# Layer 0's weight folds in fp32r halves with GpSimd butterflies, and down weights re-laid inside SBUF

## The chip, the cores and the metric

The kernel runs on one core of one Trainium2 chip. The metric is the device time of one execution in microseconds. The engines are TensorE (PE; PEld is its weight load), VectorE (DVE), ScalarE (ACT), GpSimd (POOL) and SyncE (SP), whose queue issues nearly all DMAs.

## The reference

Two layers over x of 4 x 512 tokens x 512 features. Each layer is x + s * silu(f), where s is an attention and f a feed-forward network, both of the normalised x.

- Layer 0, attention: 32 query heads of 16, 8 key heads, softmax over 512 keys.
- Layer 0, feed-forward (the part the change touches), with H a normalised Walsh-Hadamard transform:

```python
x = fwht(x * SU_ug) / SCALE                        # 512 features
x_up = x @ W_up.T * (Wscale_ug[:INTER] * SCALE)    # INTER = 2048
x_gate = x @ W_gate.T * (Wscale_ug[INTER:] * SCALE)
x = silu(x_gate) * x_up
x = fwht(x * SU_dp) / SCALE                        # 2048 features
x = x @ W_down.T * (Wscale_dp * SCALE)
```

- Layer 1: a gated delta-rule recurrence over 6 heads of 64, and a feed-forward network with the signs of its weights.

The kernel does not transform the activations of layer 0's feed-forward network. It folds the transforms into the weights once, at the start: H512 diag(SU_ug) into gate and up, H2048 diag(SU_dp) and the scales into down.

## The kernel before

**The stream.** Layer 0 is one stream of units `u` (line 532). Unit u holds maxima of scores (`maxima`, PE L418, DVE reduce L419), exponentials 11 units later (`exps`, PE L439, ACT L441), weight work from the table `early`, and from u = 16 on two halves of the feed-forward network (`half`, so `gate_up` at L326 or `down` at L344). Eight units are one set of four heads; before a set begins, `set_queries` brings its queries into `qT` by four DMAs (L405). `values` follows each set (L449 to L473). A batch has 64 units: 32 with `gate_up`, 32 with `down`. The tile framework's scheduler decides the final order of the instructions on each engine; each engine then runs its own queue in order and waits on semaphores. Layer 1 follows with its own stages.

**Gate and up weights.** There are 16 pieces n (eight groups of 256 columns, gate and up in turn). `load_raw(n)` loads 128 x 4 x 256 fp32 (three buffers `raw`). `mix(n, 0)` and `mix(n, 1)` are butterflies over the four 128-row blocks, each an add (L52) and a subtract (L53) of 128 x 512, on DVE. `fold(n, j)` multiplies two blocks each by the fp32 matrix `hs`, which is the 128-point transform times SU_ug (made by L516 to L519), and splits the result into two fp32r parts: the rounded one on ACT (L256), the rest on DVE (L257). The parts `fo` serve batch 0's `gate_up` directly and are stored to `wS` in DRAM (L262) for the other batches. `fold(n, 1)` also issues the load of raw n + 3. Chunk c of `gate_up` uses half of pieces 2(c // 2) and 2(c // 2) + 1. Its up half goes through ACT into `hT` (L336) and is multiplied there on POOL (L337).

**Down weights.** 16 tiles `stage[q]` of 128 x 512, in the buffers that `hT` uses later, hold rows 16p + q of W_down.T. `mix_down(q)` multiplies one by the 16-step part of the transform, `h16`, with a plain fp32 product (L270), copies it back (L271) and writes it to DRAM as rows of `wdt` (L272). After the last one, four DMAs read `wdt` into `wdn` with other rows on the partitions (L275). `fold_down(a)` is another fp32 product with `hmat` (L281) and a scaling on DVE (L282).

Of the kernel before, what the change touches and what calls it, by code (L numbers as in the profile page):

```python
# [10 lines left out]
F32 = mybir.dt.float32  # L11
F32R = mybir.dt.float32r
AF = mybir.ActivationFunctionType
ALU = mybir.AluOpType
# [4 lines left out]
P = 128  # L19
NB, SEQ, DM = 4, 512, 512  # L20
NT = NB * SEQ // P
TB = SEQ // P
KC = DM // P
FF = 2048
NI = FF // P
# [8 lines left out]
def kernel(ctx: ExitStack, tc: tile.TileContext, i: dict, out: bass.AP):  # L34
    nc = tc.nc

    def new(pool, shape, dtype, tag, **kw):
        return pool.tile(shape, dtype, tag=tag, name=tag, **kw)
# [9 lines left out]
    def butterfly(eng, dst, src, dim, h, pin=lambda ins: ins):  # L48

        s = src.rearrange("p (n two h) f -> p n two h f", two=2, h=h)  # L50
        d = dst.rearrange("p (n two h) f -> p n two h f", two=2, h=h)
        pin(eng.tensor_tensor(d[:, :, 0], s[:, :, 0], s[:, :, 1], ALU.add))  # L52
        pin(eng.tensor_tensor(d[:, :, 1], s[:, :, 0], s[:, :, 1], ALU.subtract))  # L53
# [24 lines left out]
    dram = ctx.enter_context(tc.tile_pool(name="dram", bufs=1, space=DRAM))  # L78
# [7 lines left out]
    sum_d = new(dram, [NB, HG, 4, SEQ], F32, "sum_d")  # L86
    rec_d = new(dram, [NB, HG, 4, SEQ], F32, "rec_d")

    wdt = new(dram, [FF, DM], F32, "wdt")

    identf = new(cst, [P, P], F32, "identf")
    make_identity(nc, identf)
# [8 lines left out]
    if True:  # L101
# [5 lines left out]
        bmm = l0.enter_context(tc.tile_pool(name="bmm", bufs=3, space=PSUM, side="right"))  # L107
        awp = l0.enter_context(tc.tile_pool(name="awp", bufs=1, side="right"))
        hp = l0.enter_context(tc.tile_pool(name="hp", bufs=2, side="right"))
        a0 = top.enter_context(tc.tile_pool(name="a0", bufs=1, side="right"))  # L110

        wdn = new(awp, [P, NI, DM], F32, "wdn")
        su_ug = new(awp, [P, KC], F32, "su_ug")
# [17 lines left out]
        inorder = tc.keep_in_program_order  # L131
# [31 lines left out]
        CQ = 2 * P  # L163
        raws, fos = {}, {}

        def load_raw(n):
            q, m = n // 2, n % 2
            raws[n] = new(a0, [P, KC, CQ], F32, "raw", bufs=3)
            nc.sync.dma_start(
                raws[n], i[("w_gateT", "w_upT")[m]][:, ts(q, CQ)].rearrange("(k p) n -> p k n", p=P)  # L170
            )
# [11 lines left out]

        stage = [new(hp, [P, DM], F32, "hT", bufs=16) for _ in range(NI)]
        for q in range(NI):
            if q in (0, 6, 12):
                load_raw(q // 6)
            nc.sync.dma_start(stage[q], i["w_downT"].rearrange("(p q) n -> q p n", q=NI)[q])


# [16 lines left out]

        hmat = identf
        for h in (8, 16, 32, 64, 1, 2, 4):
            nxt = new(a0 if h == 64 else awp, [P, P], F32, "h16" if h == 64 else "hmat", bufs=1 if h == 64 else 2)  # L210
            butterfly(nc.vector, nxt.unsqueeze(2), hmat.unsqueeze(2), P, h, inorder)
            hmat = nxt
            if h == 64:
                h16 = nxt
        inorder(nc.vector.tensor_reduce(
            mrow, identf.rearrange("p (j d) -> p j d", d=32)[:, :, 0:2], AX.XY, ALU.add
        ))
# [12 lines left out]
        def scales():  # L230
            inorder(nc.vector.tensor_scalar(hwg, wsc[:, 0, :], 0.5 / DM**0.5, None, ALU.mult))
            inorder(nc.vector.tensor_tensor(cdn, wsc[:, 0, :], wsc[:, 1, :], ALU.mult))
            nc.vector.tensor_tensor(cdn, cdn, su_dp, ALU.mult)
            nc.vector.tensor_scalar(cdn, cdn, 0.5 / DM / FF**0.5, None, ALU.mult)
# [3 lines left out]
        tmps = {}  # L238

        def mix(n, stage):  # L240
            if stage == 0:
                tmps[n] = new(a0, [P, KC, CQ], F32, "tmp")
                butterfly(nc.vector, tmps[n], raws[n], KC, 1)
            else:
                butterfly(nc.vector, raws[n], tmps[n], KC, 2)

        def fold(n, j):
            q, m = n // 2, n % 2
            if j == 0:
                fos[n] = new(a0, [P, 2, 2, KC, P], F32R, "fo", bufs=3)  # L250
            ph = new(bmm, [P, 2, CQ], F32, "mm")
            for k in range(2):
                nc.tensor.matmul(ph[:, k, :], hs[:, 2 * j + k, :], raws[n][:, 2 * j + k, :], start=True, stop=True)
            ph = ph.rearrange("p k (c n) -> p c k n", n=P)
            hi, lo = fos[n][:, :, 0, 2 * j : 2 * j + 2, :], fos[n][:, :, 1, 2 * j : 2 * j + 2, :]
            nc.scalar.copy(hi, ph)  # L256
            nc.vector.tensor_tensor(lo, ph, hi, ALU.subtract)  # L257
            if j == 0:
                return
            if n + 3 < FF // P:  # L260
                load_raw(n + 3)
            nc.sync.dma_start(  # L262
                wS[ts(q, 2), m].rearrange("c p h k n -> p c (h k n)"),
                fos[n].bitcast(F32).rearrange("p c h k n -> p c (h k n)"),
            )


        def mix_down(q):
            ph = new(bmm, [P, DM], F32, "mm")
            nc.tensor.matmul(ph, h16, stage[q], start=True, stop=True)  # L270
            nc.scalar.copy(stage[q], ph)  # L271
            nc.sync.dma_start(wdt.rearrange("(p q) n -> q p n", q=NI)[q], stage[q])  # L272
            if q == NI - 1:
                for o in range(4):
                    nc.sync.dma_start(  # L275
                        wdn[:, ts(o, 4), :], wdt[ts(o, DM), :].rearrange("(a p) n -> p a n", p=P)
                    )

        def fold_down(a):
            ph = misc()  # L280
            nc.tensor.matmul(ph, hmat, wdn[:, a, :], start=True, stop=True)  # L281
            nc.vector.scalar_tensor_tensor(wdn[:, a, :], ph, cdn[:, a : a + 1], drow, ALU.mult, ALU.mult)  # L282

        vps, kTs, oTs, hTs, g0s, wcs, ths = {}, {}, {}, {}, {}, {}, {}
# [72 lines left out]
        def misc(dtype=F32):  # L357

            return new(bpy, [P, SEQ], dtype, "y") if piece[0] % 64 < 32 else new(bmm, [P, SEQ], dtype, "mm")
# [10 lines left out]
        def halves(u):  # L370

            return 2 * (min(max(u, LATE), NU) - LATE) + max(u - NU, 0)
# [129 lines left out]
        def half(h):  # L502
            piece[0] = h // 2
            ffn(h // 2, h % 2)
# [5 lines left out]
        nc.sync.dma_start(drow, i["wsc_dp"].to_broadcast([P, DM]))  # L510
        nc.sync.dma_start(wo, i["wo0"].rearrange("(k p) n -> p k n", p=P))

        ph = new(bmm, [P, KC, P], F32, "mm")
        for k in range(KC):
            hk = new(a0, [P, P], F32, "hk", bufs=1)
            inorder(nc.vector.tensor_scalar(hk, hmat, su_ug[:, k : k + 1], None, ALU.mult))  # L516
            nc.tensor.transpose(ph[:, k, :], hk, identf)
        hs = new(a0, [P, KC, P], F32, "hs")
        nc.scalar.copy(hs, ph)  # L519

        scales()

        early = {}
        for n in range(FF // P):
            u = LATE + 2 * n - 4
            for d, f in ((-3, lambda n=n: mix(n, 0)), (-2, lambda n=n: mix(n, 1)),
                         (0, lambda n=n: fold(n, 0)), (1, lambda n=n: fold(n, 1))):
                early.setdefault(u + d, []).append(f)
        for q in range(NI):
# [2 lines left out]
        for u in range(NU + LAG + 1):  # L532
            b, r = u // 64, u % 64
            v = u - LATE
            piece[0] = halves(u) // 2
            if v == 32:
                top.close()
                zp.append(l0.enter_context(tc.tile_pool(name="zp", bufs=2, side="right")))
            if 0 < u - LAG <= NU and (u - LAG) % 8 == 0:
                values((u - LAG) // 8 - 1)  # L540
            if u < NU:
                maxima(u)
            if 0 <= u - LAG < NU:
                exps(u - LAG)
            for f in early.get(u, ()):
                f()
            for h in range(halves(u), halves(u + 1)):
                half(h)
            if u % 8 == 7 and u < NU:
                max_rows(u // 8)  # L550
            if u % 32 in (22, 23) and u + 10 < NU:
                queries((u + 10) // 64, (u + 10) % 64 // 32, u % 32 - 22)
            if u % 8 == 0 and u + 8 < NU:
                set_queries(u // 8 + 1)
            if 16 <= v < 16 + NI:
                fold_down(v - 16)
            if 0 < b < NB and r in (18, 19, 20, 21):
                layer_sum(b - 1, r - 18)
            if 0 < b < NB and r in (25, 26, 28, 29):
                norm1(b - 1, (25, 26, 28, 29).index(r))  # L560
            if b + 1 < NB:
                if r == 34:
                    load_x(b + 1)
                if r in (43, 44, 45, 46):
                    stats0(b + 1, r - 43)
                if r == 49:
                    norm0(b + 1)
                if r == 52:
                    keys_values(b + 1)
# [284 lines left out]
    total, done, n = sum(x[0] for x in steps), 0.0, 0  # L854
# [53 lines left out]
    raws = {}  # L908
# [492 lines left out]
    n = 0  # L1401
# [56 lines left out]
```

## Time and profile before

| | us |
|---|---|
| median of 3 runs | 1493.79 (1490.02 to 1494.76) |
| span of the profiled execution, first to last instruction | 1492.3 |
| median less that span | 1.5 |
| first maxima product (L418) | 18.4 |
| first product of gate_up (L326) | 43.1 |
| last product of a gate or up fold (L253) | 164.9 |
| first product of down (L344) | 183.7 |

No separate device time is listed for the profiled execution, so its span is set beside the median. An engine's busy time is a mean over stages with different limits; what an edit of the first 165 us is worth is read from that stage. Times in the lists below the page count from the span's start. A transfer's row on SPq is the time that its issue holds the queue, not the time until it lands. One fp32 product appears as two records.

### The profile page before, as it was taken

Reading aid. Unit: us, or ns where it says so; the run is one execution under the profiler, and the core shown is the slowest. Engines: PE = TensorE matmul, PEld = TensorE weight load, DVE = VectorE, ACT = ScalarE, POOL = GpSimd, SP = SyncE. Lnnn points to the kernel's source line nnn. Section 1 sums busy time; section 2 is a strip of 40 time slices with the busy share of each in tenths; the row PEclk is TensorE's granted clock in tenths of the full one; section 3 lists DMA queues with packets and bytes.
Section 4 is the critical chain, followed back from the end, with each engine's and each line's share of the span. In section 5 each row is a group of like instructions: output and inputs, shape, how many; then the busy total and the mean of one; then the engine's idle time right before and its main releaser. Section 6 shows DMA issues by size and latency. Waiting matters only on the chain. (4 is left out here: it accounts for less than half of the span.)

```text
span 1492.3 us, 22700 instructions
## 1 busy us (share of the span) xinstructions
PE 1429.4 (96%) x8144; PEld 855.6 (57%) x8144; DVE 1035.8 (69%) x1863; ACT 709.6 (48%) x1046; POOL 313.5 (21%) x304
## 2 busy tenths in 40 slices
PE   7999999999999999999999899999999999999998
PEld 3565533555335553356434576787568766776675
DVE  7999755765557655666525869768975799477746
ACT  4655554666446664466552434434353344323433
POOL 1112100322003220033100330045112531052001
PEclk9999999999999999999999999999999999999989
DMA  8865410475105741166103553434453354425532
GB/s 307 322 220 194 149 29 16 149 237 190 27 21 190 231 149 28 36 212 225 56 20 103 160 146 101 116 92 147 134 151 103 91 161 135 126 73 150 162 83 96
DMA packets 201793, 199.11 MB, mean 133 GB/s; under 512 B 65520, under 2 KB 153040, under 8 KB 200784
## 3 DMA queue, kind: packets, MB, share of 16 engines
q1 hardware_dynamic: 198624, 196.29, 41.9%
q10 hardware_dynamic: 3056, 1.37, 0.4%
q8 instruction: 64, 1.05, 0.3%
q14 instruction: 49, 0.40, 0.1%
HBM read 146.80 MB, written 46.19 MB: 129 GB/s over the span
## 5 line engine op out<-in xcount | busy, mean ns | idle before, releaser
L419 DVE TENSOR_REDUCE nmx<-sc 128x2 f32<-128x1024 f32 x256 | 312.3, 1220 | 159.1 <-PE st L439 147.3
L441 ACT ACTIVATE pe<-st 128x1024 f16<-128x1024 f32 x256 | 262.6, 1026 | 143.4 <-PE st L439 141.6
L344 PE MATMUL y<-wdn,hT 128*128 128x512 f32 x512 | 253.3, 617 | 3.0 <-DVE g L348 1.7
L326 PE MATMUL mm<-xr,wc 128*128 128x512 f32 x768 | 206.8, 410 | 0.0
L326 PEld LDWEIGHTS mm<-xr,wc 128*128 128x128 f32 x768 | 137.4, 189 | 48.4 <-issue 21.8
L337 POOL TENSOR_TENSOR hT<-hT,th 128x512 f32<-128x512 f32 x64 | 84.2, 1316 | 319.2 <-ACT hT L336 309.0
L344 PEld LDWEIGHTS y<-wdn,hT 128*128 128x128 f32 x512 | 87.0, 189 | 96.0 <-issue 88.5
L711 PE MATMUL pu<-xn1T,wp 128*128 128x512 f32 x288 | 129.9, 594 | 0.0
L941 PE MATMUL ph<-xsh,sg 128*128 128x512 f32 x256 | 113.0, 441 | 5.6 <-ACT sg L926 5.3
L418 PE MATMUL sc<-kT,qT 32*128 32x512 f16 x512 | 102.5, 385 | 7.8 <-DVE nmx L419 7.4
L926 ACT ACTIVATE sg<-sw 128x512 fp32r<-128x512 f32 x128 | 79.5, 625 | 55.2 <-PE y L972 32.2
L941 PE MATMUL ph<-xsl,sg 128*128 128x512 f32 x256 | 104.1, 407 | 0.7 <-DVE xsl L901 0.7
L418 PEld LDWEIGHTS <-qT 32*128 32x128 f16 x512 | 26.2, 91 | 131.8 <-issue 127.9
L465 POOL TENSOR_TENSOR oT<-os,sm 128x512 f16<-128x512 f32 x32 | 41.5, 1298 | 285.9 <-DMA sm<-rec_d 248.8
L439 PE MATMUL st<-qm,kT 32*128 32x512 f16 x512 | 100.0, 384 | 0.3 <-ACT pe L441 0.3
L946 ACT ACTIVATE hT<-ph,upsc 128x512 f32<-128x512 f32 x64 | 43.8, 685 | 94.3 <-PE ph L941 94.1
L711 PEld LDWEIGHTS pu<-xn1T,wp 128*128 128x128 f32 x288 | 54.0, 191 | 56.6 <-issue 54.8
L972 PE MATMUL y<-sg,hsh 128*128 128x512 f32 x256 | 83.0, 432 | 0.7 <-ACT sg L926 0.7
L1019 POOL TENSOR_TENSOR gm<-g,le 128x384 fp32r<-128x384 f32 x64 | 57.8, 921 | 83.0 <-PE pu L1020 52.0
L326 PE MATMUL mm<-xr,fo 128*128 128x512 f32 x256 | 73.2, 420 | 0.9 <-DVE fo L257 0.9
L972 PE MATMUL y<-sg,hsl 128*128 128x512 f32 x256 | 73.5, 400 | 0.0
L332 ACT ACTIVATE th<-mm,hwg 128x512 f32<-128x512 f32 x64 | 44.0, 688 | 56.0 <-PE mm L326 56.0
(302 smaller groups left out, 2370.2 us busy)
## 6 DMA issues: line engine op xcount, KB each, us to landing
wc<-wS SPq DMA_DIRECT2D x96, 512.0 KB
wS<-fo SPq DMA_DIRECT2D x16, 1024.0 KB
sw<-in_upT SPq DMA_DIRECT2D x64, 256.0 KB
sw<-in_downT SPq DMA_DIRECT2D x64, 256.0 KB
sm<-rec_d SPq DMA_DIRECT2D x128, 64.0 KB
raw<-in_w_gateT SPq DMA_DIRECT2D x8, 512.0 KB
hT<-in_w_downT SPq DMA_DIRECT2D x16, 256.0 KB
raw<-in_w_upT SPq DMA_DIRECT2D x8, 512.0 KB
```

The costliest lines, as they stand in the source:

```text
L326: nc.tensor.matmul(pgs[m], wcs[b, c, m][:, h, k, :], xrs[b][:, k, :], start=(k + h == 0), stop=(k == KC - 1 and h == 1))
L337: nc.gpsimd.tensor_tensor(hT, hT, ths[b, c], ALU.mult)
L344: nc.tensor.matmul(ys[t], hTs[b, c][:, ts(t, P)], wdn[:, c, :], start=(c == 0), stop=(c == NI - 1))
L418: nc.tensor.matmul(sc[:, j, :], qTs[n][rows, ts(t, P)], kTs[b, g // 4][rows, :], start=True, stop=True)
L419: nc.vector.tensor_reduce(nmxs[n][:, t, 2 * pr : 2 * pr + 2], sc, AX.X, ALU.max, negate=True)
L439: nc.tensor.matmul(st[:, j, :], kTs[b, g // 4][rows, ts(k, P)], qms[n][rows, :], start=True, stop=True)
L441: nc.scalar.activation(pes[u], st, AF.Exp)
L711: nc.tensor.matmul(pp, wps[b, n][:, k, 0:P], xn1Ts[b][:, k, :], start=(k == 0), stop=(k == KC - 1))
L926: tc.keep_in_program_order(nc.scalar.activation(sgs[b, c, m], raws[b, c, m], AF.Sign))
L941: ins = nc.tensor.matmul(ph, sgs[b, c, 0][:, ts(k, P)], xss[b][n][:, k, :], start=(k + n == 0), stop=(k == KC - 1 and n == 1))
L972: ins = nc.tensor.matmul(yss[b][t], hss[b, c][n][:, ts(t, P)], sgs[b, c, 1], start=(c + n == 0), stop=(c == NI - 1 and n == 1))
L1019: nc.gpsimd.tensor_tensor(gm, bc_in(s["g2"][:, t, u, x], P), bc_mid(le, 3), ALU.mult)
```

## The change

Three things change in layer 0's weight preparation.

1. The folds of gate and up, `mix_down` and `fold_down` use two fp32r products each in place of one fp32 product: `halves_of` splits the data into a rounded part on ACT and the rest (on DVE for gate and up, on POOL for down), and both are multiplied by an fp32r matrix of plus and minus one. SU_ug is applied where the fold is split (ACT with a scale, DVE with scalar_tensor_tensor, one block at a time), so `hs` and its four transposes go.
2. The butterflies of gate and up run on POOL. `raw` has two buffers and not three; raw n + 2 is loaded by `part_raw(n, 1)`.
3. The down weights change their rows by 128 transfers from SBUF to SBUF, eight per `mix_down`, each from 16 partitions into one. `fold_down` is spread over units from u = 24.

```diff
-            raws[n] = new(a0, [P, KC, CQ], F32, "raw", bufs=3)
+            raws[n] = new(a0, [P, KC, CQ], F32, "raw", bufs=2)
...
-            if q in (0, 6, 12):
-                load_raw(q // 6)
+            if q in (0, 8):
+                load_raw(q // 8)
...
         def mix(n, stage):
             if stage == 0:
                 tmps[n] = new(a0, [P, KC, CQ], F32, "tmp")
-                butterfly(nc.vector, tmps[n], raws[n], KC, 1)
+                butterfly(nc.gpsimd, tmps[n], raws[n], KC, 1)
             else:
-                butterfly(nc.vector, raws[n], tmps[n], KC, 2)
+                butterfly(nc.gpsimd, raws[n], tmps[n], KC, 2)
+
+        def halves_of(src, eng):
+            rh = new(a0, [P, 2, DM], F32R, "rh", bufs=2)
+            hi = rh[:, 0]
+            nc.scalar.copy(hi, src)
+            eng.tensor_tensor(rh[:, 1], src, hi, ALU.subtract)
+            return rh
+
+        rhs = {}
+
+        def part_raw(n, j):
+            rhs[n, j] = halves_of(raws[n][:, 2 * j : 2 * j + 2, :].rearrange("p k n -> p (k n)"), nc.vector)
+            if j == 1 and n + 2 < FF // P:
+                load_raw(n + 2)
...
             for k in range(2):
-                nc.tensor.matmul(ph[:, k, :], hs[:, 2 * j + k, :], raws[n][:, 2 * j + k, :], start=True, stop=True)
-            ph = ph.rearrange("p k (c n) -> p c k n", n=P)
-            hi, lo = fos[n][:, :, 0, 2 * j : 2 * j + 2, :], fos[n][:, :, 1, 2 * j : 2 * j + 2, :]
-            nc.scalar.copy(hi, ph)
-            nc.vector.tensor_tensor(lo, ph, hi, ALU.subtract)
+                for h in range(2):
+                    nc.tensor.matmul(ph[:, k, :], hmr, rhs[n, j][:, h, ts(k, CQ)], start=(h == 0), stop=(h == 1))
+            for k in range(2):
+                kk = 2 * j + k
+                src = ph[:, k, :].rearrange("p (c n) -> p c n", n=P)
+                hi = fos[n][:, :, 0, kk, :]
+                nc.scalar.activation(hi, src, AF.Copy, scale=su_ug[:, kk : kk + 1])
+                nc.vector.scalar_tensor_tensor(
+                    fos[n][:, :, 1, kk, :], src, su_ug[:, kk : kk + 1], hi, ALU.mult, ALU.subtract
+                )
             if j == 0:
                 return
-            if n + 3 < FF // P:
-                load_raw(n + 3)
...
         def mix_down(q):
+            rh = halves_of(stage[q], nc.gpsimd)
             ph = new(bmm, [P, DM], F32, "mm")
-            nc.tensor.matmul(ph, h16, stage[q], start=True, stop=True)
+            for h in range(2):
+                nc.tensor.matmul(ph, h16r, rh[:, h], start=(h == 0), stop=(h == 1))
             nc.scalar.copy(stage[q], ph)
-            nc.sync.dma_start(wdt.rearrange("(p q) n -> q p n", q=NI)[q], stage[q])
-            if q == NI - 1:
-                for o in range(4):
-                    nc.sync.dma_start(
-                        wdn[:, ts(o, 4), :], wdt[ts(o, DM), :].rearrange("(a p) n -> p a n", p=P)
-                    )
+            for r in range(P // NI):
+                nc.sync.dma_start(wdn[r * NI + q : r * NI + q + 1, :, :], stage[q][r : P : P // NI, :])

         def fold_down(a):
+            rh = halves_of(wdn[:, a, :], nc.gpsimd)
             ph = misc()
-            nc.tensor.matmul(ph, hmat, wdn[:, a, :], start=True, stop=True)
+            for h in range(2):
+                nc.tensor.matmul(ph, hmr, rh[:, h], start=(h == 0), stop=(h == 1))
...
+                         (-1, lambda n=n: part_raw(n, 0)), (0, lambda n=n: part_raw(n, 1)),
...
-            if 16 <= v < 16 + NI:
-                fold_down(v - 16)
+            for a in range(NI):
+                if v == 8 + 3 * a // 2:
+                    fold_down(a)
```

More of the change, by code (lines that the diff above doesn't have):

```diff
@@ L87 @@
     rec_d = new(dram, [NB, HG, 4, SEQ], F32, "rec_d")
-    wdt = new(dram, [FF, DM], F32, "wdt")
     identf = new(cst, [P, P], F32, "identf")
@@ L209 @@
         for h in (8, 16, 32, 64, 1, 2, 4):
-            nxt = new(a0 if h == 64 else awp, [P, P], F32, "h16" if h == 64 else "hmat", bufs=1 if h == 64 else 2)
+            nxt = new(a0, [P, P], F32, "hmat", bufs=2)
             butterfly(nc.vector, nxt.unsqueeze(2), hmat.unsqueeze(2), P, h, inorder)
@@ L213 @@
             if h == 64:
-                h16 = nxt
+                h16r = new(a0, [P, P], F32R, "h16r")
+                inorder(nc.vector.tensor_copy(h16r, nxt))
+        hmr = new(a0, [P, P], F32R, "hmr")
+        inorder(nc.vector.tensor_copy(hmr, hmat))
         inorder(nc.vector.tensor_reduce(
@@ L511 @@
         nc.sync.dma_start(wo, i["wo0"].rearrange("(k p) n -> p k n", p=P))
[L513 to L519, printed above, removed]
         scales()
```

## The prediction

> **What bounds the kernel now.** I read the page's busy line and slices first, then the same engines by stage, since the edit touches only the first 165 us.
>
> ```profile
> PE 1429.4 (96%) x8144; PEld 855.6 (57%) x8144; DVE 1035.8 (69%) x1863; ACT 709.6 (48%) x1046; POOL 313.5 (21%) x304
> ```
> ```profile
> 20.00:43.00 23.00, 23.00 (x81) 10.34 (x80) 19.42 (x31) 13.06 (x23) 0.00 (x0) 1.00 0.89 321
> 43.00:165.00 122.00, 114.52 (x570) 69.56 (x568) 117.45 (x167) 69.88 (x97) 22.48 (x16) 1.00 0.62 226
> ```
> The columns of the second fence are stage, length, then busy time (and instructions) of PE, PEld, DVE, ACT and POOL, clock, DMA share, GB/s. From the first weight product (18.4 us) PE is hardly idle, DVE is 96% busy during the folds, and POOL does almost nothing. So a change that frees PE and DVE could pay, if what takes over can keep up. What takes over is POOL and the SP queue, and their prices stand in these rows (groups of the window 43 to 181, one row of POOL's and one of DVE's timeline, SP's timeline, one line's instructions, one stage):
>
> ```profile
> L326 PE MATMUL mm<-xr,fo 128*128 128x512 f32 x256 | 73.2, 420 | 0.9 <-DVE fo L257 0.9
> L253 PE MATMUL mm<-raw,hs 128*128 128x256 f32 x111 | 32.7, 408 | 1.5 <-DVE fo L257 1.5
> ```
> ```profile
> 53.60 1.27 POOL L337 TENSOR_TENSOR hT<-hT,th 128x512 f32<-128x512 f32 x1 [46.87 <-ACT hT L336]
> ```
> ```profile
> 53.70 1.72 DVE L53 TENSOR_TENSOR tmp<-raw 128x512 f32<-128x512 f32 x1
> 56.48 0.68 DVE L52 TENSOR_TENSOR raw<-tmp 128x512 f32<-128x512 f32 x1
> ```
> ```profile
> 23.27 0.34 SPq L272 DMA_DIRECT2D wdt<-hT  x1
> 23.89 2.42 SPq L405 DMA_DIRECT2D qT<-qd  x4
> 26.41 4.82 SPq L272 DMA_DIRECT2D wdt<-hT  x8
> 31.32 2.43 SPq L405 DMA_DIRECT2D qT<-qd  x4
> ...
> 36.49 0.38 SPq L169 DMA_DIRECT2D raw<-in_w_upT  x1
> ```
> ```profile
> L405 SPq DMA_DIRECT2D qT<-qd x124: 507/540/1587, 23.9 to 710.4; - x124
> ```
> ```profile
> 228.50:231.00 2.50, 2.50 (x10) 0.86 (x9) 1.21 (x2) 0.67 (x1) 0.00 (x0) 1.00 0.11 25
> ```
> To see: a POOL tensor_tensor of 128x512 takes 1.27 us, DVE's 0.68; a DVE one on two SBUF tiles that meets a POOL one takes 1.72 instead of 0.68; four transfers of 16 rows from SBUF to SBUF hold the SP queue 2.42 us, 0.605 each; a raw load is issued at 36.5 us; four such transfers (16 KB each) run at 25 GB/s.
>
> **PE, DVE, ACT: what the sum of busy time would give.** Two records make one fp32 product, so pitches come from the timeline: a 512-column fp32 product takes 0.85 us in mix_down and 0.95 with its neighbour in fold_down, a 256-column one 0.39, an fp32r one of 512 columns 0.25 to 0.27. mix_down: 16 x 0.85 = 13.7 becomes 32 x 0.26 = 8.3. fold_down: 16 x 0.95 = 15.2 becomes 8.3. fold: 64 x 0.39 = 25 becomes 128 products of 256 fp32r columns, which no row shows; between half of 0.26 and all of it that is 17 to 33 us, and I take 20, since columns set the pitch of the other forms. With the four hk transposes gone (1.1 us), PE has about 18 us less to do. DVE loses 64 x 0.68 = 43.5 of butterflies, gains 32 x 0.68 = 21.8 of raw splits and some 4.5 on the folds (64 half-size pieces at about 0.41 for 32 at 0.68): 17 less. ACT gains 64 copies x 0.58 = 37 and about 6 on the folds; in 20 to 165 it was 83 of 145 busy, so it stays short of full. None of this is what ends last.
>
> **POOL.** It gets 64 butterfly halves and 32 splits of 512 elements. At 1.29 us (median of L337) that is 124 us, into a stage where it had 28 us. In the instruction order of the changed program they are mixed with the hT products, all on one queue.
>
> **SP, the step that decides.** 16 writes and 4 reads of 128 partitions become 128 transfers of 32 KB, each from 16 partitions into one. No row has that form. Nearest are the SBUF-to-SBUF transfers of 16 rows (qT, kT, oTc), which hold SP 0.605 us in a burst; cheapest are 128-partition DRAM writes at 0.34. I take 0.605. From above: if the 16 packets of one transfer into one partition went one after another, each at the speed of an engine in the last fence (25 GB/s at 0.11 of 16 engines, 14 GB/s each, 0.14 us for 2 KB), a transfer would take 2.2 us.
>
> [...]
>
> What is queued behind these transfers: 96 of them stand in SP's order ahead of the load of raw 2 (two buffers now, so weights 2 and up are loaded only after part_raw of weights 0 and up), 72 ahead of the queries of set 2. And PE's order has no gate_up before set 2's maxima (the first 24 units of maxima stand before it), before the last mix_down, and before fold 2, which needs raw 2. Step by step:
>
> 1. Head: ACT's order has the splits of stage 0 and 1 before the square root of the first normalisation. Stage 1 has 2.4 MB in front of or in it, 7.8 us at the 304 GB/s of the first 20 us, so it lands near 9; then two copies (0.58) and another table load (1.28 on the page's row for the first). The root starts near 11.3 and not at 7.8: +3.5.
> 2. The first of the 128 transfers goes out at about 26.5 (23.3 before, plus 3.2). Set 2's queries are out at 26.5 + 80 x 0.605 = 75, against 31 to 34 before. raw 2 is issued at 26.5 + 104 x 0.605 = 89 (96 transfers and two sets of queries); raw 3 and raw 4 each come 16 transfers and two other DMAs later: 100, 110. With about 4 us to land (the raw load of 36.5 landed at 42.5 under full DMA load), raw 2 is there at 93, raw 4 at 114.
> 3. POOL has run out at about 50 and waits. Butterflies of 2: 93 to 98; the last down split 100; gate_up of chunk 0 from about 101 on PE (43 before); hT 0 stands before butterfly 3 in POOL's queue and is done at 108 (two gate_up halves of 2.1 each, a fold between, ACT's copy, 1.3 on POOL); butterfly 3 ends at 113; hT 1 stands before butterfly 4 and, by the same steps, is done at 120. So weight 4 starts at 119, at the earliest with raw 4 at 114.
> 4. From there to the last butterfly POOL's order holds 71 instructions (48 butterfly halves, 10 hT, 2 oT, 11 splits): 71 x 1.29 = 91.6 us. 24 DVE splits on two SBUF tiles collide as in the row of 1.72, each holding POOL up to 0.6: 14 at most, I take 7. Last butterfly 218, its split and fold 3 more: last fold at 221.
> 5. Before, the last fold (L253) ran at 165. At that place both programs have issued the same products on PE (216 gate_up, 88 maxima, 66 exps), so what is left is equal but for fold_down: 5 x 0.95 against 6 x 0.26, 3 us less. Behind it PE is 96 to 99% busy, so the delay is kept: 221 - 165 - 3 = +53 us.
>
> The span before is 1492.3; the median of the runs is 1493.8, 1.5 above it. So 1492.3 + 53 + 1.5 = 1547.
>
> **Removed at no gain.** The way through DRAM (4 MB out, 4 MB back) was covered: wdn was loaded by about 60 us and first used at 115. Its end gives nothing. The raw loads' third buffer was cover too: without it the first loads wait on SP as above.
>
> **Rivals.**
> - *The transfers themselves are the bound, not their issue.* For it: one partition takes all 32 KB, and each transfer waits for the eighth before it. Against: the order alternates among eight partitions 16 apart, so several can be under way. If the packets enter two at a time, half of 2.2, 1.1 us each, raw 2 is issued at 26.5 + 96 x 1.1 + 8 x 0.605 = 137, raw 4 at 174, weight 4 starts at 179, the last fold runs at 281: +113, 1607. At 2.2 us it would be near +250, 1745. It decides above 0.605.
> - *SP is cheap and POOL never waits: faster.* POOL from butterfly 0 (19 us, when tmp is free) to the last one has 103 instructions, 133 us: end at 152, last fold at 155, so 10 + 3 less: 1481. It needs raw 2 issued before about 43, that is under 0.13 us for each transfer; the shortest issue of the rows above is 0.34. At 0.34 the same steps give raw 2 at 64, weight 4 at 94, last fold at 189: +21, 1515.
> - *No change.* The folds would have to end at 168, by a price between those two; the rows do not offer one.
>
> **How the numbers follow.** Forecast (issue-bound, 0.34 to 0.8): 0.62, alone 1515 to 1580, likeliest 1547. Transfer-bound: 0.28, 1580 to 1760, half of it below 1635. Faster: 0.04; within 0.3%: 0.02; some other slowing: 0.04. 0.3% (4.5 us) is about what a measurement of this kernel can tell from no change. The range 1510 to 1635 leaves out the first side (0.06) and the upper half of the transfer case (0.14).
>
> **What would show it.** Right: the SP timeline full of wdn transfers from about 26 to 110 us at about 0.6 each; raw 2 issued near 89; first gate_up product near 101; POOL idle from about 50 to 93 and then nearly full to 218; last fold near 221; equal stages behind it. Wrong: the wdn transfers done by 60 us (then POOL alone counts, and the time is near or under 1500), or spaced at over a microsecond (then 1600 and more); or POOL's pieces far from 1.29 us.

## The result, and the profile after

| | before | after |
|---|---|---|
| median, us | 1493.53 (1490.02 to 1494.76) | 1592.66 (1584.32 to 1595.35) |
| profiled execution: its time | not listed | 1594.18 |
| its span | 1492.3 | 1592.5 |
| first gate_up | 43.1 | 109.6 |
| last gate or up fold | 164.9 | 263.5 |
| first down | 183.7 | 279.3 |

The changed kernel takes 1.0661 times as long (95% interval 1.0629 to 1.0692), 99.1 us more. The last fold is 98.6 us later, and from there to the end of the span it is 1329.0 us against 1327.4, so the loss lies in the first 264 us. The page, busy times first and then the granted TensorE clock in 40 slices of 39.8 us:

```profile
PE 1450.4 (91%) x8140; PEld 866.0 (54%) x8140; DVE 1039.6 (65%) x1861; ACT 753.1 (47%) x1142; POOL 436.5 (27%) x400
PEclk8557899999999999999999999999999999999989
```

ACT has 43.5 us more and POOL 123.0, as summed beforehand (43 and 124). PE, which was to lose 18 us, shows 21 more, and all of it ahead of the last fold: 171.4 us busy in the first 264, at a mean clock of 0.77, for 147.8 in the first 165 before, at 1.00. The second line shows where the clock was lost, at half in slices 2 and 3 above all: products last longer there (one of mix_down's 794 ns at the median, 397 at the least). DVE, which was to lose 17 us, shows 3.8 more: its 32 raw splits took 31.9 us for 21.8, its 64 fold pieces 30.5 for 26.2, and the rest of the difference is not taken apart here. The stages (columns as in the prediction):

```profile
20.00:35.00 15.00, 9.30 (x43) 4.20 (x41) 7.22 (x12) 5.01 (x9) 12.32 (x10) 0.79 0.36 93
35.00:95.00 60.00, 36.17 (x101) 13.81 (x101) 25.45 (x33) 27.09 (x44) 14.03 (x12) 0.50 0.17 50
107.00:134.40 27.40, 18.14 (x72) 12.11 (x72) 9.30 (x17) 11.49 (x20) 7.68 (x7) 0.75 0.50 177
134.40:254.00 119.60, 89.55 (x404) 58.30 (x401) 83.12 (x115) 69.03 (x121) 94.48 (x73) 0.87 0.43 151
264.00:400.00 136.00, 132.87 (x652) 60.48 (x651) 88.06 (x126) 77.06 (x98) 26.10 (x21) 1.00 0.28 93
```

From 35 to 95 us no compute engine is even two thirds busy and the DMA engines are at 0.17, so something small is being waited for. From 134 to 254 no engine is full either: POOL, the busiest, works 94.5 of 119.6 us. Behind 264 PE is full again. What is waited for stands in SP's queue (start, us on the queue, line, transfer, count):

```profile
26.32 6.33 SPq L294 DMA_DIRECT2D wdn<-hT  x8
32.75 2.44 SPq L424 DMA_DIRECT2D qT<-qd  x4
35.29 41.85 SPq L294 DMA_DIRECT2D wdn<-hT  x64
77.24 2.44 SPq L424 DMA_DIRECT2D qT<-qd  x4
79.78 15.06 SPq L294 DMA_DIRECT2D wdn<-hT  x24
94.94 0.53 SPq L168 DMA_DIRECT2D raw<-in_w_gateT  x1
...
108.39 0.53 SPq L168 DMA_DIRECT2D raw<-in_w_upT  x1
```

64 transfers take 41.85 us, 0.654 each. Set 2's queries leave at 77 and raw 2 at 95. POOL, first in its waits from 60 to 110 us and then in its timeline (the bracket is the idle time before a row and what ended it):

```profile
POOL tmp L52 <- DMA raw<-in_w_gateT: 32.7, 1, 32.7
```
```profile
100.99 1.26 POOL L52 TENSOR_TENSOR tmp<-raw 128x512 f32<-128x512 f32 x1 [32.68 <-DMA raw<-in_w_gateT]
...
116.65 1.26 POOL L356 TENSOR_TENSOR hT<-hT,th 128x512 f32<-128x512 f32 x1 [9.33 <-ACT hT L355]
...
133.22 1.26 POOL L356 TENSOR_TENSOR hT<-hT,th 128x512 f32<-128x512 f32 x1 [10.31 <-ACT hT L355]
134.44 1.26 POOL L52 TENSOR_TENSOR tmp<-raw 128x512 f32<-128x512 f32 x1
```

So POOL stands for 32.7 us on raw 2, then for 9.3 and 10.3 us on hT 0 and 1, and starts piece 4 at 134.4. The products themselves, as groups (busy us, mean ns) over 0 to 330 us:

```profile
L345 PE MATMUL mm<-xr,fo 128*128 128x512 f32 x256 | 78.4, 449 | 0.4 <-ACT hT L355 0.3
L270 PE MATMUL mm<-rh,hmr 128*128 128x256 f32 x128 | 30.3, 349 | 14.8 <-ACT rh L252 12.1 <-DVE rh L253 1.1 <-DVE th L352 0.8
```

Before, the same 256 gate_up products took 73.2 us. PE now stood idle 14.8 us in front of fold products, mostly for ACT's copy of raw.

### The profile page after: what moved, and what is told of

Read it like the earlier page. It is cut to its first block, busy times and chain, and to the rows that moved or that the text cites. A ratio compares the mean times of both kernels' runs of the same rounds, so it can differ in the third digit from the quotient of the medians.

```text
span 1592.5 us, 23069 instructions
## 1 busy us (share of the span) xinstructions
PE 1450.4 (91%) x8140; PEld 866.0 (54%) x8140; DVE 1039.6 (65%) x1861; ACT 753.1 (47%) x1142; POOL 436.5 (27%) x400
## 5 line engine op out<-in xcount | busy, mean ns | idle before, releaser
L345 PE MATMUL mm<-xr,wc 128*128 128x512 f32 x768 | 205.6, 409 | 0.0
L437 PE MATMUL sc<-kT,qT 32*128 32x512 f16 x512 | 108.5, 403 | 26.6 <-DVE nmx L438 26.1
L458 PE MATMUL st<-qm,kT 32*128 32x512 f16 x512 | 104.9, 394 | 12.3 <-ACT pe L460 11.8
L939 ACT ACTIVATE sg<-sw 128x512 fp32r<-128x512 f32 x128 | 79.5, 625 | 61.7 <-PE y L985 32.2
L345 PE MATMUL mm<-xr,fo 128*128 128x512 f32 x256 | 78.4, 449 | 0.4 <-ACT hT L355 0.3
```

The costliest lines, as they stand in the source:

```text
L345: nc.tensor.matmul(pgs[m], wcs[b, c, m][:, h, k, :], xrs[b][:, k, :], start=(k + h == 0), stop=(k == KC - 1 and h == 1))
L437: nc.tensor.matmul(sc[:, j, :], qTs[n][rows, ts(t, P)], kTs[b, g // 4][rows, :], start=True, stop=True)
L458: nc.tensor.matmul(st[:, j, :], kTs[b, g // 4][rows, ts(k, P)], qms[n][rows, :], start=True, stop=True)
L939: tc.keep_in_program_order(nc.scalar.activation(sgs[b, c, m], raws[b, c, m], AF.Sign))
```

## The experiments

The first gate_up and the last fold serve as marks: at the last fold every version has issued the same gate_up, maxima and exps products, but for 4 exps in e3_fp32r_only; the number of down folds differs by up to three, and e12_fill has its 64 extra products. e3_fp32r_only keeps the two raw buffers, which came with part 2, so that their price stands in its row and not in that of e6_before_pool. All times are us.

| run | what it is | median | over before | ratio, 95% interval | first gate_up | last fold |
|---|---|---|---|---|---|---|
| e5_before_transfers | part 3 alone | 1558.71 | +62.8 | 1.0382 to 1.0457 | 42.2 | 227.3 |
| e6_before_pool | part 2 alone, three raw buffers | 1501.42 | +5.5 | 1.0018 to 1.0064 | 47.7 | 167.5 |
| e3_fp32r_only | part 1 alone, two raw buffers | 1553.32 | +57.4 | 1.0356 to 1.0417 | 68.0 | 220.5 |
| e1_dram | parts 1 and 2 | 1557.31 | +61.4 | 1.0377 to 1.0440 | 80.7 | 231.5 |
| e10_fp32_mix | e1_dram, mix_down in fp32 | 1533.26 | +38.0 | 1.0217 to 1.0294 | 53.8 | 205.6 |
| e12_fill | e1_dram, 64 filler products | 1560.42 | +65.2 | 1.0396 to 1.0474 | 77.6 | 226.8 |
| e11_raw3 | e1_dram, three raw buffers | 1546.50 | +51.3 | 1.0298 to 1.0384 | 78.7 | 218.5 |
| e13_down_fp32 | e1_dram, fold_down in fp32 | 1547.78 | +52.5 | 1.0316 to 1.0385 | 80.8 | 217.6 |
| e8_two_queues | after, transfers on two queues | 1626.16 | +129.9 | 1.0852 to 1.0906 | 163.5 | 299.4 |
| e9_raw_on_act | after, raw loads on ACT's queue | 1660.38 | +164.1 | 1.1073 to 1.1125 | 81.0 | 329.3 |
| e14_pool_late | before, butterflies of 2 to 15 on POOL | 1498.01 | +1.8 | 0.9999 to 1.0033 | 44.1 | 165.5 |
| e16_folds_only | e10, e11 and e13 together | 1504.09 | +7.8 | 1.0044 to 1.0095 | 50.2 | 177.7 |

### Which part costs it

Theory: SP's queue, held by the 128 transfers, makes raw 2 and all behind it late. Rivals: POOL's load and the two raw buffers, or the transfers' own speed. Four runs undo a part or make one alone. e1_dram undoes part 3:

```diff
-            for r in range(P // NI):
-                nc.sync.dma_start(wdn[r * NI + q : r * NI + q + 1, :, :], stage[q][r : P : P // NI, :])
+            nc.sync.dma_start(wdt.rearrange("(p q) n -> q p n", q=NI)[q], stage[q])
+            if q == NI - 1:
+                for o in range(4):
+                    nc.sync.dma_start(
+                        wdn[:, ts(o, 4), :], wdt[ts(o, DM), :].rearrange("(a p) n -> p a n", p=P)
+                    )
```

> The changed kernel with part 3 undone: the down weights go through DRAM again (16 writes, 4 reads); fp32r folds, POOL butterflies and two raw buffers stay. Theory (the 128 transfers hold the SP queue, and raw 2 behind them starts everything late): raw 2 is issued near 52, the first gate_up product runs near 55 (109.6 in the changed kernel), the granted PE clock stays near 1 there, the last fold product comes at 190 to 205 (263.5), and the time is 1592.7 less 60 to 75: 1518 to 1533. Rival A (POOL's 124 us of work and the two raw buffers set the pace, the transfers only fill a wait): the last fold stays at 240 or later, 1570 or more. Rival B (the transfers cost all of it): last fold near 165 and 1494 or less.

1557.31, 35 us under the changed kernel. No theory's numbers hold: the last fold moves by 32 us, half of what the theory of the queue asked for, the clock falls to 0.50 here too (shown below), and 61 us stay without a single such transfer.

e3_fp32r_only also puts the butterflies back on DVE (`nc.gpsimd` to `nc.vector` in both calls of `mix`), so part 1 is left with its two buffers.

> Part 1 of the change alone, with its two raw buffers: fp32r folds, butterflies back on DVE, down weights through DRAM. Theory (parts 2 and 3 cost what is lost): DVE has 22 + 4.5 us more than before (raw splits and half-size fold pieces) in a stage where it was 96% busy, so the last fold comes 10 to 27 us later than 164.9, at 175 to 192: 1504 to 1521. Rival (two buffers or the fp32r form itself cost most of the 99): 1550 or more. A third way (fewer PE us decide): under 1490.

1553.32. The theory falls here: part 1, which I had held to be beside the path, costs 57 us by itself, with its two buffers. Some of it is the cause that the theory named, DVE's added work, for DVE is full in its later stages:

```profile
165.00:190.00 25.00, 22.19 (x96) 12.48 (x95) 25.00 (x37) 16.58 (x28) 8.48 (x6) 0.89 0.45 158
```

But the first gate_up is 25 us late already, and e1_dram is no faster, although DVE works only 107 of its 151 us from the first gate_up to the last fold (136 of 152.5 here).

e5_before_transfers is the kernel before with the two removed lines of the diff above in place of its lines for DRAM.

> The kernel before with part 3 of the change alone: 128 transfers from SBUF to SBUF in place of the way through DRAM; three raw buffers, fp32 folds, DVE butterflies. Theory (SP queue): transfers at 0.6 to 0.66 us each, the queries of set 2 out at 70 to 78 (31 to 34 before), raw 3 behind 104 transfers at 88 to 95; the butterflies of 3 wait for it, and the last fold comes at 164.9 + 30 to 55, so 1524 to 1549. Rival (the transfers only fill a wait that POOL or the buffers make): within 10 us of 1494. Third (the transfers are bound by the one partition they enter): pitch over 1 us, and over 1560.

1558.71. Its SP queue:

```profile
32.27 41.66 SPq L271 DMA_DIRECT2D wdn<-hT  x64
74.02 2.44 SPq L399 DMA_DIRECT2D qT<-qd  x4
76.56 21.54 SPq L271 DMA_DIRECT2D wdn<-hT  x32
98.21 0.52 SPq L167 DMA_DIRECT2D raw<-in_w_upT  x1
```

The pitch is again 0.651 and set 2's queries leave at 74, as the theory said; the time came 10 us above its range, since I had let the first three pieces absorb part of the delay. They absorb none: raw 3 is issued at 98.2 where it was 36.5, 61.7 later, the last fold is 62.4 later and the time 62.8. Here the mechanism of the prediction is seen without parts 1 and 2: 128 transfers on one in-order queue cost what they delay.

e6_before_pool is the kernel before with `nc.gpsimd` in both calls of `mix`.

> The kernel before with part 2 of the change alone: the butterflies of gate and up on POOL; three raw buffers, fp32 folds, way through DRAM. Theory: POOL gets 64 halves at 1.27 to 1.29 us = 82 us from about 19 on, in a stage of 146 us where it had 22 us; DVE loses 43 us; nothing waits long, so the last fold comes at 150 to 170: 1479 to 1500. Rival (POOL's pace and its hT products in the same queue cost 20 to 40 us by themselves): 1514 or more.

1501.42, 1 us above the theory's range. POOL's pace is no heavy cost when its loads come early. So parts 1, 2 and 3 cost 57, 5 and 63 us alone, 125 in sum, and 99 in the changed kernel: parts 1 and 3 each hold back the same stage with a wait of their own, and partly cover each other.

### What in part 1 costs 57 us

Three things came with it: the split chain of mix_down, two raw buffers, and fold_down's splits. PE in e1_dram, just before its clock falls, and two stages of it:

```profile
32.70 0.79 PE L293 MATMUL mm<-rh,h16r 128*128 128x512 f32 x1 [3.94 <-POOL rh L255]
```
```profile
20.00:35.00 15.00, 8.88 (x44) 3.96 (x42) 7.39 (x13) 4.85 (x9) 11.52 (x10) 0.90 0.41 119
35.00:50.00 15.00, 12.11 (x24) 4.26 (x23) 5.20 (x5) 6.77 (x13) 8.80 (x8) 0.50 0.32 124
```

A mix_down product, which before needed only its tile, now waits 3.94 us for a split on POOL, which stands in POOL's queue behind the butterflies of pieces 0 and 1. e10_fp32_mix takes the chain away:

```diff
-            rh = halves_of(stage[q], nc.gpsimd)
             ph = new(bmm, [P, DM], F32, "mm")
-            for h in range(2):
-                nc.tensor.matmul(ph, h16r, rh[:, h], start=(h == 0), stop=(h == 1))
+            nc.tensor.matmul(ph, h16, stage[q], start=True, stop=True)
```

> e1_dram (parts 1 and 2, way through DRAM) with mix_down as one plain fp32 product again; the fp32r folds of gate, up and down stay. e1_dram has its first gate_up at 80.7 us, its last fold at 231.5 and 1557. Theory (the splits of mix_down, ACT's copy and POOL's rest behind the butterflies of 0 and 1, starve PE at 26 to 33 us; its granted clock then falls to 0.50, which stretches what follows): the clock stays at 0.9 to 1.0 from 20 to 65 us, the first gate_up runs at 45 to 58, the last fold at 197 to 210, 1522 to 1536. Rival (raw 2, which has two buffers and so is loaded after part_raw(0, 1), sets the first gate_up): first gate_up at 70 or later, 1545 or more.

1533.26, 24 us less, inside the theory's range, with both marks in their place; the clock, 0.89, 0.97 and 0.80 in the three stages from 20 to 65 us, is mended less than it said. The second of the two stages above:

```profile
35.00:50.00 15.00, 12.03 (x48) 4.85 (x46) 11.86 (x18) 8.61 (x17) 5.11 (x4) 0.97 0.81 274
```

In the same busy time PE ran 48 records in place of 24 (an fp32 product counts two: mix_down's 16 were 32 records before), at clock 0.97 and not 0.50. Is the clock the cause or the sign? e12_fill holds it up by force:

```diff
             ph = new(bmm, [P, DM], F32, "mm")
+            for _ in range(4):
+                nc.tensor.matmul(ph, h16r, xrs[0][:, 0, :], start=True, stop=True)
```

> e1_dram with four extra fp32r products of 512 columns at the head of each mix_down, 64 in all, whose result is overwritten: 17 us more for PE at full clock, and nothing else changed. Theory (the halved clock is itself a cost): the clock stays above 0.9 from 20 to 65 us and the first gate_up comes 8 to 15 us earlier than 80.7 in spite of the extra work: 1543 to 1550. Rival (the clock is only a sign of PE waiting; ACT and POOL set the pace): first gate_up within 4 us of 80.7 or later, 1553 to 1575.

```profile
35.00:50.00 15.00, 14.96 (x64) 8.46 (x64) 10.68 (x17) 8.64 (x16) 7.71 (x6) 0.96 0.47 164
```

In this stage the clock stays at 0.96, yet the first gate_up comes only 3.1 us earlier and the time is not better (1560.42 against 1557.31). But PE is now full here, with the fillers: they used up what the clock gave. And they hold it for this stage only:

```profile
50.00:65.00 15.00, 10.85 (x39) 5.16 (x39) 10.17 (x16) 12.31 (x19) 7.71 (x6) 0.72 0.26 91
```

The theory asked for 0.9 up to 65 us. So this run shows that fillers gained nothing, and not what a full clock alone is worth: how much of e10's 24 us is clock and how much is the wait itself stays open.

e11_raw3 loads raw 2 at the start and raw n + 3 from `part_raw`:

```diff
-            raws[n] = new(a0, [P, KC, CQ], F32, "raw", bufs=2)
+            raws[n] = new(a0, [P, KC, CQ], F32, "raw", bufs=3)
...
-            if j == 1 and n + 2 < FF // P:
-                load_raw(n + 2)
+            if j == 1 and n + 3 < FF // P:
+                load_raw(n + 3)
```

> e1_dram with three raw buffers, raw 2 loaded at the start and raw n + 3 by part_raw, as in the kernel before. From the first gate_up to the last fold e1_dram takes 151 us, the kernel before 122. Theory (two buffers make each piece wait for its load): that stretch falls to 125 to 135, 1530 to 1542. Rival (POOL, ACT and PE hold one another in their queues: hT products, fold_down's splits and butterflies): the stretch stays at 143 or more, 1549 or more.

1546.50: 11 us less (its profiled execution took 1552.5, the most of the four), and the stretch from first gate_up to last fold falls from 151 to 140, between the two. The third buffer matters, but it is not the whole. e13_down_fp32 puts fold_down back:

```diff
-            rh = halves_of(wdn[:, a, :], nc.gpsimd)
             ph = misc()
-            for h in range(2):
-                nc.tensor.matmul(ph, hmr, rh[:, h], start=(h == 0), stop=(h == 1))
+            nc.tensor.matmul(ph, hmat, wdn[:, a, :], start=True, stop=True)
```

> e1_dram with fold_down as one plain fp32 product again: 16 POOL splits of 1.27 us (20 us) and 16 ACT copies less, PE 16 x 0.95 for 32 x 0.26, 7 us more. Theory (these splits stand in POOL's queue among butterflies and hT products, and PE waits for them: 11.8 + 9.0 us on its row of rh in that stretch): the last fold comes 10 to 20 us earlier than 231.5, 1537 to 1548. Rival (PE's own work is the limit there): 7 us more or no change, 1555 to 1565.

1547.78, 9.5 us less with 7 us more of product time: at the edge of the theory's range, its last fold (13.9 us earlier) well within it. The waits of e1_dram from 80 to 231 us that went away with it (us, times, longest):

```profile
PEld y L306 <- POOL rh L255: 11.8, 7, 2.8
PE y L306 <- POOL rh L255: 9.0, 6, 2.5
```

e16_folds_only makes all three edits at once.

> e1_dram with the edits of e10_fp32_mix, e11_raw3 and e13_down_fp32 together: what is left of the change is the gate and up folds as two fp32r products each, with their splits, and the butterflies on POOL. Alone the three edits brought 24, 11 and 9.5 us. Theory (three separate waits, at different places of the stage, so they add up): first gate_up near 50 to 55, last fold at 181 to 193, 1557 less 38 to 46: 1511 to 1519; the 12 to 20 us that stay over the kernel before are the folds' own splits (e6_before_pool, without them, is at 1501). Rival (one wait takes the place of another): 1522 or more. Other rival (the folds' splits are free, all else was the three waits): 1503 or less.

1504.09: 53 us less than e1_dram, in time more than the 44.5 of the three alone. At the last fold, though, the three alone brought 25.9, 13.0 and 13.9 us, 52.8 in sum, and all at once bring 53.8. So the waits add up there, as the theory said, and do not take one another's place; the theory's time was 7 us too long because its sum was made of times. Behind the last fold the profiled executions of e11_raw3 and e13_down_fp32 took 1332.2 and 1331.0 us where e1_dram took 1324.0, and no view here says why. What is left of the change, fp32r folds of gate and up with their splits and POOL's butterflies, stands 7.8 over before, and e6_before_pool had 5.5 of that without the folds, with an interval that overlaps. So the theory's 12 to 20 us for the folds' splits were too many, and the other rival, at 1503 or less, missed by 1 us only. The stage from 43 to 165 us:

```profile
43.00:165.00 122.00, 106.79 (x523) 63.59 (x521) 105.07 (x153) 83.31 (x143) 90.77 (x66) 0.92 0.65 228
```

PE was busy 114.5 us of it before. All engines now have slack, so what is left there is waits and not one engine's work.

### Issue or transfer, and the load's place

e8_two_queues issues the transfers alternately:

```diff
-                nc.sync.dma_start(wdn[r * NI + q : r * NI + q + 1, :, :], stage[q][r : P : P // NI, :])
+                (nc.sync, nc.scalar)[r % 2].dma_start(wdn[r * NI + q : r * NI + q + 1, :, :], stage[q][r : P : P // NI, :])
```

> The changed kernel, with every second of its 128 transfers issued by ACT's queue in place of SP's. In the changed kernel they go out one each 0.654 us and move about 50 GB/s. Theory (the issue on one queue sets that pitch): on SP the pitch stays at 0.6 to 0.7 for half as many, so set 2's queries are out near 52 (77.2) and raw 2 near 60 (94.9); ACT pays 64 issues. First gate_up 80 to 95 (109.6), 1560 to 1582. Rival (the one partition that a transfer enters, or the transfers ahead of it, set the pitch): SP's pitch doubles to about 1.3, set 2's queries and raw 2 stay where they are within 6 us, 1588 or more. A third way (transfers in ACT's in-order queue hold up its copies for mix_down): 1593 to 1630.

1626.16: the third way. A burst on both queues, SP's wait of 20 to 160 us, and the burst as a stage:

```profile
66.90 8.72 SPq L294 DMA_DIRECT2D wdn<-hT  x8
```
```profile
67.20 8.94 ACTq L294 DMA_DIRECT2D wdn<-hT  x8
76.19 1.14 ACT L252 CAST rh<-hT 128x512 fp32r<-128x512 f32 x2 [8.46 <-DMA wdn<-hT]
```
```profile
SPq L294 <- DMA wdn<-hT: 25.4, 23, 2.5
```
```profile
67.20:76.10 8.90, 1.03 (x5) 0.00 (x0) 1.23 (x1) 0.53 (x1) 0.00 (x0) 0.50 0.21 52
```

Each queue needs 1.1 us for a transfer, and both together move 52 GB/s where one alone moved 50. On one queue SP waited only 0.6 us in all for earlier transfers; on two it waits 25.4. In the changed kernel a transfer waits for the DMA that stands eight before it: the eighth `wdn` transfer stood 1.5 us for the load of `wo`, eight before it on SP and without data in common. So issue sets the pitch of one queue; with two, SP waits 23 times for earlier transfers, up to 2.5 us, so the transfers' own landing lies hardly higher, and a second queue buys next to nothing. Whether more transfers under way at a time would go faster, no run tried. The second queue costs much: ACT's copies wait behind its share (8.5 us in the row shown), and mix_down stops.

e9_raw_on_act issues the later raw loads from ACT:

```diff
-            nc.sync.dma_start(
+            (nc.sync if n < 2 else nc.scalar).dma_start(
                 raws[n], i[("w_gateT", "w_upT")[m]][:, ts(q, CQ)].rearrange("(k p) n -> p k n", p=P)
```

> The changed kernel, with the loads of raw 2 to 15 issued by ACT's queue and no longer behind the transfers on SP's; the transfers and set 2's queries stay. Theory (raw 2's place behind 96 transfers is what starts POOL late): raw 2 is issued before 70 (94.9), butterfly 2 before 75 (101.0), the first gate_up at 80 to 92 (109.6), last fold at 230 to 245 (263.5), 1558 to 1575. Rival (set 2's queries, out at 77, and the chain of mix_down's splits hold PE just as long): the first gate_up stays above 100, 1582 or more.

1660.38. raw 2 was issued at 57.5 and the first gate_up ran at 81.0, as the theory said, but the time is 85 us beyond its range. SP's waits from 20 to 160 us tell why: the transfers themselves now waited for the loads:

```profile
SPq L294 <- DMA raw<-in_w_gateT: 27.9, 1, 27.9
SPq L424 <- DMA raw<-in_w_gateT: 21.5, 2, 12.3
SPq L294 <- DMA raw<-in_w_upT: 11.7, 1, 11.7
```

These loads stand on ACT's queue, so the wait for an earlier DMA, seen with `wo` above on one queue, reaches across the two. A load that ACT issues late in its order so held transfers on SP that have no data in common with it, by 27.9 us at the longest; set 2's queries left at 144 us. The run says that raw 2's place holds the first gate_up back from 81 to 109.6. At 81 something else holds it: POOL is done with butterfly 2 at 66, and e1_dram and e11_raw3, which issue raw 2 at 61.1 and 14.4, have their first gate_up at 80.7 and 78.7. With mix_down in one product (e10_fp32_mix) it runs at 53.8, so in e1_dram mix_down's chain is what stands there, and most likely here too. What an early raw 2 would be worth to the whole, the run does not say.

### A try at a version faster than both

e14_pool_late leaves the first two butterflies on DVE, where a half takes 0.68 us for POOL's 1.27:

```diff
-                butterfly(nc.vector, tmps[n], raws[n], KC, 1)
+                butterfly(nc.vector if n < 2 else nc.gpsimd, tmps[n], raws[n], KC, 1)
...
-                butterfly(nc.vector, raws[n], tmps[n], KC, 2)
+                butterfly(nc.vector if n < 2 else nc.gpsimd, raws[n], tmps[n], KC, 2)
```

> The kernel before with the butterflies of pieces 2 to 15 on POOL, those of 0 and 1 left on DVE; nothing else of the change. With all of them on POOL (e6_before_pool) the first gate_up came at 47.7 (43.1 before), because a half takes 1.27 us on POOL and 0.68 on DVE, and the stretch to the last fold took 119.8 (121.8 before). Theory: the first gate_up is back at 43 to 44 and the stretch stays near 120, so 1490 to 1494, 2 to 6 us under the kernel before. Rival (DVE and POOL on the same two SBUF tiles hold each other up, or hT's products queue behind butterflies): 1497 or more.

1498.01, ratio 1.0016 (0.9999 to 1.0033): no gain that can be told from nothing, and inside the rival's 1497 or more. The first gate_up is back at 44.1, 3.6 us earlier than in e6_before_pool; the time is 3.4 lower, but the two intervals overlap. What DVE is freed of buys nothing, and why not was not looked into. No run here beats the kernel before.

## Why the prediction was right, and where it was short

The direction, the place and the queue were right; the likeliest time, 1547, was 46 us short. The pitch, 0.654, lay within the 0.34 to 0.8 of the issue-bound case, yet that case's range of 1515 to 1580 does not hold the result. The wide range, 1510 to 1635, does, and that is luck: its upper part stood there for the transfer-bound rival, whose cause was not the one. Step by step:

1. Head: the first transfer at 26.32 for 26.5. Right, though the square root itself ran at 12.76 for 11.3, a miss that the transfer does not show.
2. SP: 0.654 us a transfer for 0.605. Set 2's queries at 77.2 for 75, raw 2 at 94.9 for 89, landed and in use at 101.0 for 93. The 16-row transfer was the right neighbour, 8% low. The burst moved 50 GB/s over 42 us, and since each transfer waits for the DMA eight before it, no more than eight were under way.
3. The serial steps to piece 4: first gate_up at 109.6 for 101, hT 0 done at 117.9 for 108, hT 1 at 134.5 for 120, piece 4 at 134.4 for 119. This step missed 15 us, 8 of them from step 2. One more is the prediction's own slip: with hT 1 ahead of it in POOL's queue and done at 120, piece 4 could not start at 119. The products were reckoned at full clock; eight gate_up products take 2.1 us at full clock and took 3.62 us here at 109.6. The largest miss lies between butterfly 3 and hT 1, 11.6 us for 7: there too gate_up ran slowly (3.19 us for seven at 124.3), and from 127.4 to 130.4 PE did values, fold and exps products before the second half. How these share the rest was not taken apart.
4. POOL's stage: **this step failed**. Its work was sized well, 94.5 us for 98.6 with collisions (the 0.6 us that one may hold POOL up was an estimate; the longest POOL row of the stage took 1.76 us, the shortest 1.26). But it took 119.6, because the step let POOL run without a pause, and it paused 25 us, nearly all of it 8.8 on ACT's hT, 5.2 on ACT's copies for the splits, 4.4 behind DVE's fold pieces, and 5.5 on raw loads that again stand in SP's order behind other waits. From the last butterfly to the last fold it took 9.8 us for 3. Together 27 us.
5. Equal work behind the last fold: right. The 3 us from fold_down do not show (98.6 at the last fold, 99.1 in the time).

15.4 and 27.1 make the 42.5 us between 221 and 263.5.

Deeper than a size is what stood before the steps: "None of this is what ends last", of PE, DVE and ACT. It put part 1 at nothing without a reason beyond busy time. The sums of busy time were read as the cost of part 1. But with POOL's butterflies and without a transfer it costs 61 us, of which three waits were shown: mix_down's chain through ACT and POOL (24), the missing third buffer (11), fold_down's splits in POOL's queue (10), and 53 when all three go. In the changed kernel they lie partly under SP's wait (the parts alone sum to 125 us, together they cost 99), so a prediction from SP alone came within 46 us. That "the raw loads' third buffer was cover" was right. That the end of the way through DRAM gives nothing is not contradicted, and not shown: no run takes that way out without the transfers.

The rivals: the transfer-bound case gives 1607 at 1.1 us each, near the result in its number but not in its cause, since the pitch was 0.654. The fast case needed transfers under 0.13 us.

## What to carry to other kernels

An fp32 product split in two fp32r ones was cheaper in PE's time in the gate and up folds (30.3 us for 37.7) and dearer in mix_down (22.4 for 15.8), most of which ran at half clock, and it puts two more engines in front of each product; where PE is fed in order, count the chain and whose queue the split stands in, not the microseconds. A row of small DMAs costs the delay of whatever is queued behind it: here 128 transfers at 0.65 us moved one load by 62 us, and the time by 63. When a stage is to be bound by a newly loaded engine, allow for its waits: a sum of work that is right to 5% was 21 us short here.

## What the runs showed of the hardware

- In e3_fp32r_only the clock fell without a long idle gap, and 8 us of a nearly full PE did not bring it back. PE never stood idle for over 1.01 us between 26 and 32 us (it was busy 50 to 67% of each 2 us), yet the clock was at 0.50 from 32 on, and stayed there through four windows in which PE was nearly full:

```profile
34.00:36.00 2.00, 1.77 (x4) 0.79 (x3) 0.74 (x1) 0.82 (x3) 1.60 (x2) 0.50 0.41 158
36.00:38.00 2.00, 1.99 (x5) 0.64 (x5) 0.21 (x1) 1.46 (x3) 1.57 (x2) 0.50 0.37 143
38.00:40.00 2.00, 1.98 (x5) 0.65 (x5) 1.01 (x1) 1.28 (x3) 1.17 (x2) 0.50 0.31 119
40.00:42.00 2.00, 1.97 (x6) 0.68 (x4) 1.63 (x2) 1.01 (x3) 1.04 (x1) 0.50 0.41 148
```

  In e1_dram the clock fell to 0.50 within a gap of 3.94 us. The busy time here counts a product until its modelled end, so short gaps may hide in it.
- DVE's splits of raw on two SBUF tiles took a median of 949 ns beside POOL's work in the changed kernel (681 at the least, 1809 at the most).
- Issuing on a second queue raised the rate of SBUF-to-SBUF transfers into single partitions from 50 to 52 GB/s only.
